# Layer 2 of a four-layer convolution network: the order of ScalarE's squares, the two relus and the projection within a turn

## The chip, the cores and the metric

The kernel runs on one core of one Trainium2 chip. The metric is the time of one execution on the device in microseconds (us); the median of three executions of the kernel before is 8452.17 us (8451.48 to 8460.17). The core has five engines that run side by side, each working through its own instructions in order: TensorE (PE, with its weight loads apart as PEld), VectorE (DVE), ScalarE (ACT), GpSimd (POOL) and SyncE (SP). SP computes nothing here; it issues all of the kernel's transfers between memory and the core. Engines wait for each other and for transfers by semaphores.

## The reference

The input x has 16 images of 64 x 64 pixels with 256 channels. Four layers follow each other, each as x + layer(norm(x)): a linear attention, a channel and spatial gate with a state scan and a batch norm, a 3 x 3 involution (layer 2 in this text, the third in order) and a 7 x 7 involution (layer 3). What matters here, cut to layer 2 and its neighbours:

```
# layer 1 ends: x2 is the gated map, normed over the batch, with a relu
x = x + relu((x2 - mean) * rsqrt(var + EPS) * bn_gamma + bn_beta)
# layer 2: v = group norm of x (32 groups, mean and variance per image)
r  = relu(((v @ Wr + br) - mean) * rsqrt(var + BN_EPS) * gamma + beta)  # kernel branch, 64 wide
w  = (r @ Ws + bs)            # 9 weights for each of 16 groups and each pixel
xi = v @ Wi + bi              # projection, 256 channels, zero-padded by one pixel
out[pixel, c] = sum over the 9 neighbours k of w[pixel, group(c), k] * xi[neighbour k, c]
x = x + out
# layer 3 begins with the group norm of this x
```

Everything is float32.

## The kernel before

Layer 2's stage is one long list of turns, written out by hand inside `tc.manual_schedule()` (line 1204): each engine carries out its instructions in the order in which the program names them. An image is cut into eight chunks of 512 pixels (NCH, CT). In turn n four jobs run on four different chunks, by the lags of line 1184, `LAG = (0, 12, 20, 31)`, with the function `jobs` (1187) turning a turn's number into images and chunks:

- *end* (lag 0): layer 1's last step, `end_of_layer1` (965), a generator in three parts. VectorE makes two multiplies (975, tiles z and pf); ScalarE takes the relus of both (981) and GpSimd adds them to x1, which gives x2 (985), and x2's store is noted; ScalarE squares x2 with a running sum (992, tile sq). When an image's last chunk is squared, `norm2` is begun (999): the group norm of the image in small steps, one step at each call of `step()`, which also scales the layer's weights by the norm.
- *proj* (lag 12): `projected` (1031). TensorE multiplies x2 by the projection (1038, px), ScalarE writes it with its bias into pad (1042), a padded image with one row of border; the last chunk of an image also copies two border rows (1049, 1050).
- *inv* (lag 20): the involution. One turn ahead of it, `prepare` (1236) makes what it needs: `reduced2` (1052) is the kernel branch's product (1059, pr) and relu (1062, rt); `patches` (1075) transposes the padded lines on TensorE (1084, pt) and copies them in nine pieces on ScalarE (1088, xs), with the first half of the weights (1069, pw) made behind the first three copies through the argument `between`. In its own turn VectorE multiplies patches and weights in two halves (`products`, 1107, pd), the first half is summed on GpSimd (1120, 1121) and the second on VectorE (1261), and the residual, transposed by TensorE (`residual`, 1093, lo), is added by VectorE (1231 for the first half, in the next turn, and 1263 for the second). The result is x3.
- A turn later (*made*), `turned` (1123) transposes x3 back (1133) and ScalarE copies it with a running sum (1134, c3), and `statistics3` (1150) squares it on ScalarE (1154). An image's last chunk begins `norm3` (1161), the same small steps for layer 3's norm.
- *cen* (lag 31): `centred` (1172) loads x3 again, subtracts the group means on GpSimd (880, cen) and notes twelve stores to strips, the layout that layer 3 reads.

The image's first patches need the border rows that the projection of the same image's last chunk writes. So in the turn before an image's first involution chunk (an *image's first turn* in the change's words, `nxt[1] == 0`), `prepare` stands behind `projected`, and in all others ahead of it.

SP issues, in each turn: loads for the next turn (942: x2p, x2r, two of x1, two of pf), stores noted in the turn before (1213: x2, twelve of strips, two of x3, two of c3), and four loads of xc for the next turn's centring (942). Tiles are double-buffered, x2r and x3 threefold. TensorE's results for px, pr, pt and the norms' small products share three PSUM buffers (tag tr).

ScalarE's order in an ordinary turn before is: two relus of layer 1, the kernel branch's relu, nine xs copies, two c3 copies, two pads, layer 3's two squares, layer 1's two squares. In an image's first turn it is: two relus of layer 1, two c3 copies, two pads with the border copies, the kernel branch's relu, nine xs copies, four squares.

Of the kernel before, what the change touches and what calls it, by code (L numbers as in the profile page):

```python
# [19 lines left out]
NCH = 8  # L20
# [16 lines left out]
def network(ctx: ExitStack, tc: tile.TileContext, a: dict, out: bass.AP):  # L37
    nc = tc.nc
    NI = a["x"].shape[0]
# [859 lines left out]
    with ExitStack() as st:  # L899
# [29 lines left out]
        for b in range(2):  # L929

            rt = bconst(f"rt{b}", [65, CT])
# [33 lines left out]
        def end_of_layer1(i, rc):  # L965

            if rc == 0:
                st0[i] = [
                    wk.tile([P, 2, NCH], F32, tag=f"st0{k}", name="st0") for k in range(2)
                ]  # L970
            sums, squares = st0[i]
            x1, pf = taken("x1"), taken("pf")
            zs = [wk.tile([P, 2, 256], F32, tag="z", name="z", bufs=1), pf]
            for h, z in enumerate(zs):
                nc.vector.scalar_tensor_tensor(
                    z, x1[:, h], ngm1[:, i, h : h + 1], pf, ALU.add, ALU.mult
                )
            yield
            x2 = wk.tile([P, 2, CT], F32, tag="x2", name="x2")
            for h, z in enumerate(zs):  # L980
                nc.scalar.activation(
                    z, z, AF.Relu, bias=bnp[:, 1, h : h + 1], scale=ab[:, 0, i, h : h + 1],
                    accum_out=sums[:, h, rc : rc + 1],
                )
                nc.gpsimd.tensor_tensor(
                    x2[:, h].rearrange("p (t g) -> p g t", g=2), z, x1[:, h], ALU.add
                )
            stores.append((x2_d[i, rc], x2))
            yield
            sq = wk.tile([P, CT], F32, tag="sq", name="sq", bufs=1)  # L990
            for h in range(2):
                nc.scalar.activation(
                    sq, x2[:, h], AF.Square,
                    bias=ngm1[:, i, h : h + 1], accum_out=squares[:, h, rc : rc + 1],
                )
            if rc == NCH - 1:
                begun.append(norm2(i))
# [54 lines left out]
        def reduced2(i, rc):  # L1052

            wrs, b2, _, _ = gn2[i]
            rt = rts[rc % 2]
            x2 = taken("x2r")
            pr = tr.tile([P, CT], F32, tag="tr", name="pr")
            for h in range(2):
                nc.tensor.matmul(
                    pr[0:64, :], lhsT=wrs[:, h, :], rhs=x2[:, h], start=(h == 0), stop=(h == 1)  # L1060
                )
            nc.scalar.activation(rt[0:64, :], pr[0:64, :], AF.Relu, bias=b2, scale=sb2[0:64, 0:1])  # L1062
            return x2, rt

        def weights(rt, oh):

            pw = pwp.tile([P, 4, 72], F32, tag="pw", name="pw")
            for r in range(4):
                nc.tensor.matmul(
                    pw[:, r], lhsT=rt[:, r * P : (r + 1) * P], rhs=ws[:, oh * 72 : oh * 72 + 72],  # L1070
                    start=True, stop=True,
                )
            return pw

        def patches(i, rc, between):


            xs = xs_p.tile([P, 6, 3, C], F32, tag="xs", name="xs")
            for j in range(3):
                for e in range(0, 6, 2):  # L1080
                    pt = tr.tile([P, 2, C], F32, tag="tr", name="pt")
                    for k in range(2):
                        for h in range(2):
                            nc.tensor.transpose(  # L1084
                                pt[:, k, h * P : (h + 1) * P],
                                lines[:, h, rc * 4 + e + k, 2 * j : 2 * j + P], ident,
                            )
                    nc.scalar.copy(xs[:, e : e + 2, j, :], pt)  # L1088
                if j == 0:
                    between()  # L1090
            return xs
# [31 lines left out]
        def turned(i, rc, x3):  # L1123

            if rc == 0:
                st3[i] = [
                    wk.tile([P, 2, NCH], F32, tag=f"st3{k}", name="st3") for k in range(2)
                ]
            c3 = wk.tile([P, 2, 2, 256], F32, tag="c3", name="c3", bufs=2)
            for oh in range(2):  # L1130
                pt = tr.tile([P, 4, P], F32, tag="tr", name="pt")
                for r in range(4):
                    nc.tensor.transpose(pt[:, r, :], x3[:, r, oh * P : (oh + 1) * P], ident)
                nc.scalar.activation(
                    c3[:, oh], pt.rearrange("p r t -> p (r t)").rearrange("p (t g) -> p g t", g=2),
                    AF.Copy, accum_out=st3[i][0][:, oh, rc : rc + 1],
                )
            x3n = x3_d[i].rearrange("(g r w) c -> g w r c", g=2, w=HW)
            for g in range(2):
                stores.append((x3n[g][:, rc * 4 : rc * 4 + 4], x3[g:P:2]))  # L1140
            for h in range(2):
                stores.append((
                    c3_d[i, :, h].rearrange("p (g t) -> p g t", g=2)[
                        :, :, rc * 256 : rc * 256 + 256
                    ],
                    c3[:, h],
                ))
            return c3
# [23 lines left out]
        def centred(i, rc):  # L1172
            cen = wk.tile([P, 4, 4, 64], F32, tag="cen", name="cen")
            stores.extend(centred_strips(i, rc, taken("xc"), cen, gmb[i]))
# [6 lines left out]

        LAG = (0, 12, 20, 31)
        TURNS = NI * NCH + 23

        def jobs(n):

# [14 lines left out]

        with tc.manual_schedule():
            loads(0)
            ahead, made = None, None
            for n in range(TURNS):
                end, proj, inv, cen = jobs(n)
                nxt = jobs(n + 1)[2]
                done, stores[:] = list(stores), []  # L1210
                loads(n + 1)
                for dst, src in done:
                    nc.sync.dma_start(out=dst, in_=src)
                nxt_cen = jobs(n + 1)[3]
                if nxt_cen:
                    load_centred(*nxt_cen)
                now, ahead = ahead, None
                ending = end_of_layer1(*end) if end else None
                if ending:
                    next(ending)  # L1220
                    next(ending)
                if cen:
                    centred(*cen)
                step()
                for c in begun:
                    next(c)
                chains.extend(begun)
                begun.clear()
                if made:
                    half = made[2][:, :, 0:P]  # L1230
                    nc.vector.tensor_tensor(half, half, made[3], ALU.add)
                if inv:
                    w1 = weights(now[1], 1)
                    x3 = wk.tile([P, 4, C], F32, tag="x3", name="x3", bufs=3)

                def prepare():
                    x2r, rt = reduced2(*nxt)
                    ahead = [x2r, rt]
                    ahead.append(patches(*nxt, lambda: ahead.append(weights(rt, 0))))
                    return ahead  # L1240

                if nxt and nxt[1]:
                    ahead = prepare()
                if inv:
                    los = residual(now[0])
                c3 = turned(*made[:3]) if made else None
                step()
                if proj:
                    projected(*proj)
                if inv:  # L1250
                    pd = products(0, now[2], now[3])
                    sums_on_pool(pd, x3)
                if nxt and not nxt[1]:
                    ahead = prepare()
                if inv:
                    pd1 = products(1, w1, now[3])
                step()
                if made:
                    statistics3(*made[:2], c3)
                if inv:  # L1260
                    nc.vector.tensor_reduce(x3[:, :, P:C], pd1, AX.X, ALU.add)  # L1261
                    half = x3[:, :, P:C]
                    nc.vector.tensor_tensor(half, half, los[1], ALU.add)
                if ending:
                    next(ending, None)
                made = (*inv, x3, los[0]) if inv else None
            for dst, src in stores:
                nc.sync.dma_start(out=dst, in_=src)
# [380 lines left out]
```

## Time and profile before

| What | Value |
|---|---|
| Median of three executions | 8452.17 us (8451.48 to 8460.17) |
| The profiled execution | 8439.31 us; its span 8437.5 us |
| Busy share of the span | PE 82%, PEld 63%, DVE 71%, ACT 58%, POOL 36% |
| Layer 2's first turns, end alone or end and projection | 3419 to 3555 us |
| Its involution, from the first product to the last | 3555.7 to 6028 us |
| The two products of a turn (L1107), each | 4.95 us |
| The sum of the second half (L1261) | 4.95 us |
| The sums on GpSimd of a turn (L1120, L1121) | 8.4 to 8.5 and 1.6 to 2.0 us |
| A layer-1 relu (L981), a square (L992), each with its sum read | 0.99 us, 0.91 us |
| The kernel branch's relu (L1062), an xs copy (L1088), a pad (L1042) | 0.76 us, 0.59 us, 0.69 us |
| Granted TensorE clock, mean of the span | 0.903 |

The span is the time from the first instruction to the last one of a single profiled execution. Busy is time in which an engine has an instruction of its own under way; an engine's idle time is put down to what it waited for last. A line of the profile names the source line (L1107), the engine, the operation, and the tiles as out<-in; "SPq" is SP's queue, and its entries are the issue of a transfer, not the transfer itself.

### The profile page before, as it was taken

The page shows a single profiled execution, that of the slowest core. Times are in us where ns is not written, and L with a number is a line of the kernel's source. Part 1 is how long each engine was busy: PE and PEld are TensorE (multiplying, and loading weights), DVE is VectorE, ACT ScalarE, POOL GpSimd, SP SyncE. Part 2 cuts the span into 40 slices and gives each one's busy share as a digit, 9 for nine tenths or more (in the row PEclk, how much of TensorE's full clock was granted, in tenths as well). Part 3 has the DMA queues.
Part 4 walks back from the last instruction along what each step waited for, and adds up shares of the span by engine and source line. Part 5 has one row for each costly group of instructions (what it writes and reads, how often), then busy time and mean ns, then how long its engine had stood idle before and what let it go on. Part 6 is the DMA issues. An engine that isn't in the chain of part 4 may idle for free.

```text
span 8437.5 us, 214993 instructions
## 1 busy us (share of the span) xinstructions
PE 6919.5 (82%) x88348; PEld 5293.7 (63%) x88348; DVE 6026.7 (71%) x7071; ACT 4858.5 (58%) x11136; POOL 3065.7 (36%) x2154
## 2 busy tenths in 40 slices
PE   7888888888888776487887888788588888888887
PEld 5666666666666542265665565566477777777776
DVE  6877887787777757499999999999644444444444
ACT  3655655555565437676666666665355555555554
POOL 1222222222222100377777777777511211111112
PEclk9999999999999868688888888889699999999999
DMA  7644444434333228657777777776578788888887
GB/s 223 191 143 138 138 133 146 140 130 137 131 117 113 98 72 265 223 201 233 241 238 242 238 238 239 238 237 211 188 227 254 247 250 255 254 258 256 258 253 244
DMA packets 1081768, 1695.65 MB, mean 201 GB/s; under 512 B 138833, under 2 KB 684962, under 8 KB 1079634
## 3 DMA queue, kind: packets, MB, share of 16 engines
q1 hardware_dynamic: 1080786, 1681.90, 62.0%
q8 instruction: 696, 11.40, 0.6%
q14 instruction: 286, 2.34, 0.1%
HBM read 1234.54 MB, written 469.76 MB: 202 GB/s over the span
## 4 chain that ended last, share of the span: by engine, by line
PE 49%; DVE 19%; DMA 11%; ACT 9%; issue 7%; SPq 3%; POOL 2%; DVEq 0%; ACTq 0%; POOLq 0%
PE pk L1366 13%; PE pa L1432 8%; PE pkv L292 4%; PE pt L1084 4%; PE px L1038 4%; DMA x<-x_d 3%; DVE pd L1107 3%; PE py L423 2%; PE pq L280 2%; DMA xn<-in_x 2%; PE pctx L350 2%; PE pr L1333 2%; ACT sq L432 1%; DVE mq L387 1%; DVE x L451 1%
## 5 line engine op out<-in xcount | busy, mean ns | idle before, releaser
L1107 DVE TENSOR_TENSOR pd<-xs,pw 128x4608 f32<-128x4608 f32 x256 | 1255.8, 4946 | 42.2 <-ACT xs L1088 42.2
L1366 PE MATMUL pk<-rt,span 64*128 64x176 f32 x12288 | 1186.6, 330 | 48.4 <-issue 41.3
L1376 ACT ACTIVATE wm<-pk,spanb 128x176 f32<-128x176 f32 x2560 | 846.0, 424 | 569.0 <-PE pk L1366 566.8
L1452 POOL TENSOR_TENSOR ex<-ex,rx 128x192 f32<-128x192 f32 (+2 forms) x768 | 436.4, 570 | 1854.8 <-DVE ex L1445 1198.3
L1120 POOL TENSOR_TENSOR pd<-pd 128x2048 f32<-128x2048 f32 (+2 forms) x384 | 1075.9, 2802 | 75.6 <-DVE pd L1107 55.4
L1366 PEld LDWEIGHTS pk<-rt,span 64*128 64x128 f32 x12288 | 977.7, 193 | 129.7 <-issue 71.9
L1445 DVE SCALAR_TENSOR_TENSOR ex<-pa,msk,ex 128x192 f32<-128x192 f32 x704 | 294.3, 418 | 1040.3 <-ACT ex L1444 976.1
L292 PE MATMUL pkv<-wq,xn 128*128 128x256 f32 x4096 | 968.9, 382 | 14.5 <-ACT va L301 14.5
L1084 PE MATMUL pt<-ident,pad 128*128 128x128 f32 x4608 | 756.3, 330 | 266.7 <-ACT rt L1062 266.7
L375 POOL TENSOR_TENSOR qa<-qa,mq 128x1024 f32<-128x1024 f32 x256 | 507.5, 2005 | 1170.8 <-DVE mq L384 511.5
L1084 PEld LDWEIGHTS pt<-ident,pad 128*128 128x128 f32 x4608 | 673.9, 175 | 407.2 <-ACT rt L1062 292.6
L1381 DVE TENSOR_TENSOR wm<-pk,spanb 128x704 f32<-128x704 f32 x896 | 793.9, 888 | 189.3 <-PE pk L1366 186.4
L1432 PE MATMUL pa<-wm,xw 126*32 126x48 f32 x45056 | 754.9, 215 | 211.5 <-issue 185.6
L292 PEld LDWEIGHTS pkv<-wq,xn 128*128 128x128 f32 x4096 | 772.7, 192 | 227.1 <-issue 101.3
L1432 PEld LDWEIGHTS pa<-wm,xw 126*32 126x32 f32 x45056 | 623.5, 112 | 391.8 <-issue 333.2
L1088 ACT COPY xs<-pt 128x512 f32<-128x512 f32 x1152 | 619.4, 591 | 239.4 <-PE pt L1084 233.8
L1261 DVE TENSOR_REDUCE x<-pd 128x512 f32<-128x4608 f32 x128 | 633.4, 4949 | 2.2 <-DVE gm L140 0.3
L1038 PE MATMUL px<-x2p,wis 128*128 128x512 f32 x1024 | 519.3, 653 | 111.8 <-issue 63.8
L280 PE MATMUL pq<-xn,wq 128*128 128x512 f32 x1024 | 526.2, 629 | 95.1 <-DVE xn L166 77.1
L423 PE MATMUL py<-wo,o 128*128 128x256 f32 x2048 | 527.6, 413 | 32.3 <-DVE maps L510 28.6
L423 PEld LDWEIGHTS py<-wo,o 128*128 128x128 f32 x2048 | 488.9, 310 | 65.3 <-issue 39.1
L1444 ACT ACTIVATE ex<-pa,msk 128x192 f32<-128x192 f32 x704 | 299.4, 425 | 388.6 <-PE pa L1432 189.1
(234 smaller groups left out, 11879.3 us busy)
## 6 DMA issues: line engine op xcount, KB each, us to landing
xw<-strips SPq DMA_DIRECT2D x1408, 256.0 KB
xn<-in_x SPq DMA_DIRECT2D x256, 512.0 KB
x_d<-x SPq DMA_DIRECT2D x256, 512.0 KB
xin<-in_x SPq DMA_DIRECT2D x128, 512.0 KB
x<-in_x SPq DMA_DIRECT2D x128, 512.0 KB
xm<-x_d SPq DMA_DIRECT2D x128, 512.0 KB
x<-x_d SPq DMA_DIRECT2D x128, 512.0 KB
x<-x_d SPq DMA_DIRECT2D x256, 256.0 KB
```

What stands on the lines that cost most here:

```text
L280: nc.tensor.matmul(pq, lhsT=wq[:, h, f0 : f0 + P], rhs=xn[:, h], start=(h == 0), stop=(h == 1),)
L292: nc.tensor.matmul(pkv[:, q], lhsT=xn[:, h, q * P : (q + 1) * P], rhs=wq[:, h, f0 + P : f0 + 384], start=(h == 0), stop=(h == 1),)
L423: nc.tensor.matmul(py[:, q, :], lhsT=om[i, hf][:, :, ch * 4 + q], rhs=wo[:, hf, :], start=(hf == 0), stop=(hf == 1),)
L1038: nc.tensor.matmul(px, lhsT=w[:, h, fh * P : (fh + 1) * P], rhs=x2[:, h], start=(h == 0), stop=(h == 1),)
L1084: nc.tensor.transpose(pt[:, k, h * P : (h + 1) * P], lines[:, h, rc * 4 + e + k, 2 * j : 2 * j + P], ident,)
L1107: nc.vector.tensor_tensor(pd.rearrange("p r (g f) k -> p r g f k", f=16), run, pw.rearrange("p r (g k) -> p r g k", k=9).unsqueeze(3).broa ...
L1120: nc.gpsimd.tensor_tensor(pd[..., 0:n], pd[..., 0:n], pd[..., n : 2 * n], ALU.add)
L1261: nc.vector.tensor_reduce(x3[:, :, P:C], pd1, AX.X, ALU.add)
L1366: nc.tensor.matmul(pkv[:, b, m], lhsT=span[half, first + gg, s0 : s0 + P], rhs=rto[half, o // 4 * 2 + m, :], start=True, stop=True,)
L1376: nc.scalar.activation(dst[:, m // 2, m % 2], pkv[:, m // 2, m % 2], AF.Identity, bias=spanb[:, g0 + m : g0 + m + 1],)
L1381: nc.vector.tensor_tensor(dst, pkv, spanb[:, g0 : g0 + 4].rearrange("p (b m) -> p b m", b=2).unsqueeze(3).broadcast_to([P, 2, 2, NTL]), AL ...
L1432: nc.tensor.matmul(pav[p0 : p0 + 32, :, tj * TC : (tj + 1) * TC].rearrange("c g (w v) -> c g w v", v=2), lhsT=xw[0:TILE_IN, k, tj, 32 * q ...
```

## The change

The lags of projection, involution and centring grow by one, and one turn is added. Layer 1's squares of a chunk (`squares`) now run one turn after its relus: behind the first three xs copies of `patches` and the weights' first half ("the heads"), or, where there is nothing to prepare, behind the relus. In an ordinary turn the kernel branch's relu (in `reduced2`) comes first on ScalarE, and layer 1's relus, with GpSimd's sums and the centring, follow it (`relus`, called from `prepare`). In an image's first turn the order is: relus, projection, preparation, and then the residual and the turned chunk. Layer 3's squares follow directly on `turned`, ahead of the projection's pads. GpSimd's sums of the first half stay before the second product.

```diff
-        LAG = (0, 12, 20, 31)
-        TURNS = NI * NCH + 23
+        LAG = (0, 13, 21, 32)
+        TURNS = NI * NCH + 24
...
-            ahead, made = None, None
+            ahead, made, ending = None, None, None
...
-                ending = end_of_layer1(*end) if end else None
+                squares, ending = ending, end_of_layer1(*end) if end else None
                 if ending:
                     next(ending)
-                    next(ending)
-                if cen:
-                    centred(*cen)
                 step()
...
-                def prepare():
+                def relus():
+                    if ending:
+                        next(ending)
+                    if cen:
+                        centred(*cen)
+
+                def prepare(other):
                     x2r, rt = reduced2(*nxt)
+                    other()
                     ahead = [x2r, rt]
-                    ahead.append(patches(*nxt, lambda: ahead.append(weights(rt, 0))))
+
+                    def between():
+                        ahead.append(weights(rt, 0))
+                        if squares:
+                            next(squares, None)
+
+                    ahead.append(patches(*nxt, between))
                     return ahead
 
-                if nxt and nxt[1]:
-                    ahead = prepare()
+                first = nxt and not nxt[1]
+                if first:
+                    relus()
+                    projected(*proj)
+                    ahead = prepare(lambda: None)
+                elif nxt:
+                    ahead = prepare(relus)
+                else:
+                    relus()
+                    if squares:
+                        next(squares, None)
                 if inv:
                     los = residual(now[0])
-                c3 = turned(*made[:3]) if made else None
+                if made:
+                    statistics3(*made[:2], turned(*made[:3]))
                 step()
-                if proj:
+                if proj and not first:
                     projected(*proj)
                 if inv:
                     pd = products(0, now[2], now[3])
                     sums_on_pool(pd, x3)
-                if nxt and not nxt[1]:
-                    ahead = prepare()
-                if inv:
                     pd1 = products(1, w1, now[3])
                 step()
-                if made:
-                    statistics3(*made[:2], c3)
                 if inv:
                     nc.vector.tensor_reduce(x3[:, :, P:C], pd1, AX.X, ALU.add)
                     half = x3[:, :, P:C]
                     nc.vector.tensor_tensor(half, half, los[1], ALU.add)
-                if ending:
-                    next(ending, None)
                 made = (*inv, x3, los[0]) if inv else None
```

## The prediction

> **What bounds the kernel now.** The change touches layer 2 alone, and there I read four views in this order: busy time by stretch, VectorE's waits, SP's queue in order of time, and SP's own waits. Layer 2's products run from 3555.7 to 6028 us. Its long middle, where all its jobs overlap, is turns 44 to 123 (ten images of eight turns, from one stalled first product to another, 4013.7 to 5627.4). Busy time there (columns: stretch, length, then busy us of PE, PE weight loads, VectorE, ScalarE, GpSimd, granted clock, DMA share, GB/s):
>
> ```profile
> 4013.70:5627.40 1613.70, 1287.31 (x6642) 964.20 (x6642) 1514.85 (x821) 1046.80 (x2301) 1219.39 (x580) 0.85 0.73 239
> ```
>
> A turn takes 1613.7/80 = 20.17 us, and VectorE is busy for 94% of it. That suggests that VectorE binds and that its remaining waits are the price. Its waits there (us in total, times, longest):
>
> ```profile
> DVE pd L1107 <- ACT xs L1088: 32.2, 10, 4.0
> DVE isq L93 <- PE pv L151: 14.3, 10, 1.8
> DVE mom L114 <- ACT sq L992: 10.0, 10, 1.5
> DVE mom L114 <- ACT sq L1154: 9.3, 9, 1.8
> ```
>
> The diff aims at lines 1, 3 and 4: 51.5 us. But VectorE's need is well below 20.17 us. Undisturbed turns (21, 22, 26) take 17.55 us, and the two group norms add some 3 us per image: 8 x 17.55 + 3 = 143 us, where an image takes 161.4. The rest is about 8 us of waits and about 10 us of VectorE instructions that run long: the two layer-1 multiplies of a turn (L975) take 0.75 us each when alone and up to 2.0 beside GpSimd's sums. So something else sets 20.17. SP's queue, one turn of it:
>
> ```profile
> 4455.11 0.40 SPq L942 DMA_DIRECT2D x2p<-x_d  x1
> 4455.56 0.43 SPq L942 DMA_DIRECT2D x2r<-x_d  x1
> 4456.10 1.31 SPq L942 DMA_DIRECT2D x<-x_d  x2
> 4457.51 1.09 SPq L942 DMA_DIRECT2D pf<-fac_d  x2
> 4458.64 0.65 SPq L1213 DMA_DIRECT2D x_d<-x  x1
> 4459.41 10.39 SPq L1213 DMA_DIRECT2D strips<-cen  x12
> 4469.91 1.30 SPq L1213 DMA_DIRECT2D x_d<-x  x2
> 4471.31 1.10 SPq L1213 DMA_DIRECT2D c_d<-c  x2
> 4472.46 2.62 SPq L942 DMA_DIRECT2D xc<-x_d  x4
> 4475.18 0.40 SPq L942 DMA_DIRECT2D x2p<-x_d  x1
> ```
>
> 27 transfers follow each other without a hole, and the next turn's x2p comes 20.07 us after this one's. The transfers carry eight semaphores in rotation, and each waits until the one eight places before has landed. SP's waits in the same ten images:
>
> ```profile
> SPq L1213 <- DMA xc<-x_d: 62.7, 106, 1.2
> SPq L1213 <- DMA x2r<-x_d: 47.9, 80, 1.6
> SPq L1213 <- DMA x2p<-x_d: 46.2, 78, 1.4
> ...
> SPq L942 <- PE px L1038: 2.4, 4, 0.7
> ```
>
> SP waits for its own transfers (157 us, 2 per turn). The remaining rows, some 78 us in pieces of at most 1.4 us, mostly name engine work that no transfer touches (copies of xs, rt), so I take them for landings put down to a neighbour. The one engine whose work a load needs shows 2.4 us in 80 turns. SP is saturated, and no engine holds it up. How that reaches VectorE (GpSimd in order of time):
>
> ```profile
> 4479.81 2.36 POOL L880 TENSOR_TENSOR cen<-xc,gmb 128x1024 f32<-128x1024 f32 x1 [4.07 <-DMA x2p<-x_d]
> 4482.12 8.44 POOL L1120 TENSOR_TENSOR pd<-pd 128x2048 f32<-128x2048 f32 x3
> 4490.64 1.97 POOL L1121 TENSOR_TENSOR x<-pd 128x512 f32<-128x512 f32 x1
> ```
>
> xc, SP's last load of a turn, was issued by 4475.08 and landed 4.7 us later; then cen, then the sums, until 4492.61; VectorE adds the residual (L1231) at 4493.09 and may multiply from 4493.8. So a turn's products can't begin before 18.7 us after the last issue of xc. Set against that floor, the products of turns 36 to 126 start 0.0 to 6.4 us after it, never before. Each image touches the floor (0.0 to 1.3 us above) in its turn 3 mod 8, is thrown up by the xs wait, and sinks back. SP's own turn length doesn't follow that distance: 20.22 us in 19 turns within 1 us of the floor, 20.15 in 27 turns more than 4 us above it.
>
> **What the Trainium skill says.** "Perfetto Trace Analysis", section What "DMA-bound" means, lists as a separate bound the sequencer that issues, recognised by a track of solid DMA slices, which are descriptor generation and not movement. This trace agrees: SP solid, DMA share only 0.73. "SBUF — State Buffer", section Who interferes with whom, says that a VectorE instruction with two SBUF inputs contends with GpSimd's reads: here 0.75 against up to 2.0 us (L975). "DMA: Bandwidth & Descriptors", section Issuing engines are not separate DMA queues, says that issue time is usually small beside the transfer; here the measurement says otherwise, 0.67 us of issue for strips pieces of 36 to 128 KB.
>
> **The change part by part.** No instruction and no transfer is added or removed; SP's and GpSimd's orders within a turn are the old ones (x2's store, strips, x3 and c3; sums into x2, cen, products' sums).
>
> *First turns (line 3 of PE's order).* Before, PE in turn 67 waited for the residual's PSUM and then 5.19 us more until px at 4484.04 (VectorE's L1028 had just read the small result before it), so xs was complete at 4498.2 and the products came 4.05 us late. Now px follows w1 and the relus. Relus end at 4474.3, px done by then, two pads of 0.69 and two edge copies of 0.31 end at 4476.3; rt 0.76, nine copies at 0.59 to 0.85, 1.82 of squares: about 4484 to 4487, before the floor at 4493.8. Wait gone: 32.2 us in ten images. What is late next there is L1231, held by GpSimd's sums at the floor.
>
> *Squares.* The layer-1 squares (2 x 0.91 us) go behind the first three copies of the next turn, and layer 3's pair in front of the pads, into ScalarE's idle time before them (301.5 us in 80 turns waiting for px, 3.8 a turn). The moments (L114) then find them done: 19.3 us gone. Behind the squares are six xs copies and PE's transposes; they end about 10 us before the next products in ordinary turns, and that covers 1.82 us. Without this cover it would be 1.82 a turn.
>
> *Kernel branch's relu first.* rt needs only PE's pr; it now precedes the layer-1 relus, of which the x2 sums on GpSimd and so cen are waiting. In turn 63 ScalarE reached the relus at 4413.6 through 3.6 us of squares; now pr ends at 4412.3, rt near 4413.0, and the multiply at 4412.5. Relus no later: zero, covered by the removed squares, else 0.76 a turn.
>
> *One turn more.* Projection, products and centring each lag one turn further behind layer 1. A filling turn costs (3549.39 - 3443.34)/18 = 5.9 us; a full turn of 20.2 drops out, since layer 1's and centring's loads overlap in one turn less; one draining turn of 16.1 (turns 136 and 137) is added: +1.8.
>
> *What is left as a gain.* Before SP fills up (turns 20 to 31) VectorE does bind: waits of the moments 0.42 + 0.35 + 1.20 = 2.0 us. SP's waits for px, 2.4 x 95/80 = 2.9 us over some 95 full turns. The other savings only bring VectorE down to the floor earlier. Sum: +1.8 - 2.0 - 2.9 = **-3.1 us** against the profiled execution's 8439.3 us (span 8437.5), so 8436; carried to the median, 12.9 higher, **8449 us**.
>
> Unknown: whether landings come sooner or later with engines in other phase. The two means above differ by 0.07 us, so I take none, and +-0.1 us a turn, x 95 = +-10, as its bounds. With the spread of the runs (8451.5 to 8460.2), the likeliest case has 8434 to 8466.
>
> **Rivals.** *A: VectorE binds after all.* For it: 94% busy, and the chain of waits runs through ScalarE and PE too. Then the waits are saved, 51.5, and the long multiplies of the turn after each first turn, 10 x 1.8 = 18: 69.8 x 97/80 = 85 us, 2.0 before, and the extra turn costs 5.9 - 1.5: about 8370. Against it: the floor, and SP's indifference. If SP's landing waits shrank in part, the time lies between.
>
> *B: slower, through SP's head.* The load of x2p for turn n+1 waits until px of turn n-1 has read its buffer. Near the floor px ended 9 us before SP got there (4466 against 4475.18); 6 us above it they meet (4516.27 and 4516.29, turn 69). ScalarE's pads now come behind 1.8 us of squares. If px is held 1.8 us longer and VectorE still rides high in four turns of eight, SP loses 1.8 x 4 x 12 = 86 us, half of it 43: 8495. It decides from px held past SP's arrival by 0.18 us in the mean turn (17 us). Against: without the xs wait VectorE doesn't ride high.
>
> *C: the edit misses.* xs stays late in first turns because the relus, put first, wait for VectorE's multiplies. Costless at the floor: 8452, as now.
>
> **How the numbers follow.** Forecast 0.62, C 0.06, A with its part gains 0.20, B 0.12. 0.2% is 17 us, about what a measurement here can tell from none: faster 0.20, same 0.68, slower 0.12. The range: the likeliest's 8434 to 8466, down to 8400 for part gains and up to 8476 for a small B.
>
> **What would show it.** Right: VectorE's waits for xs and for the squares nearly gone, its waits for GpSimd's sums (7.7 us in these ten images) and cen's waits for DMA larger, SP's turn still 20.0 to 20.3 us, products within about 2 us of the floor throughout. A is right if SP's turn falls below 19.5; B if SP waits for px in many turns. I am wrong altogether if SP shows holes and VectorE's waits still vanish.

## The result, and the profile after

The changed kernel takes 8463.99 us (median of 12 executions, 8445.27 to 8477.87); the kernel before, on the same chip, 8457.28 us (12 executions, 8446.66 to 8462.88). The ratio is 1.0009, with a 95% interval of 1.0000 to 1.0018, so a difference of 0.2% lies outside it. The forecast was 8449 with "no change" at 0.68.

The same ten images as before (turns of the middle, here from 4036.8 to 5647.4 us), busy time by stretch (stretch, length, then busy us of PE, PE weight loads, VectorE, ScalarE, GpSimd, granted clock, DMA share, GB/s):

```profile
4036.80:5647.40 1610.60, 1243.08 (x6640) 889.82 (x6640) 1555.68 (x822) 1023.82 (x2301) 1230.89 (x581) 0.89 0.72 239
```

A turn takes 1610.6/80 = 20.13 us, where it took 20.17. What stands out is VectorE: busy for 1555.7 us instead of 1514.9, with the same work. Its waits in this stretch (us in total, times, longest):

```profile
DVE b L1026 <- PE pm L1020: 24.7, 9, 4.2
DVE x L1228 <- POOL x L1121: 9.2, 6, 1.5
DVE gmb L869 <- PE pb L864: 8.0, 10, 0.8
DVE isq L93 <- PE pv L151: 0.9, 2, 0.6
```

The waits for xs and for the two kinds of squares are gone, and the one for pv fell from 14.3 to 0.9. A new one has come: the norm's small result b waits for pm, which TensorE now makes behind an image's first patches. So 65 us of waits were saved and 25 came. SP's queue, one turn in order of time:

```profile
4499.34 2.61 SPq L942 DMA_DIRECT2D xc<-x_d  x4
4502.05 0.40 SPq L942 DMA_DIRECT2D x2p<-x_d  x1
...
4507.02 9.77 SPq L1213 DMA_DIRECT2D strips<-cen  x12
4516.90 1.28 SPq L1213 DMA_DIRECT2D x_d<-x  x2
4518.27 1.10 SPq L1213 DMA_DIRECT2D c_d<-c  x2
4519.43 2.63 SPq L942 DMA_DIRECT2D xc<-x_d  x4
```

It is as solid as before: xc comes back after 20.09 us. SP's own waits in the ten images, where no row names px any more:

```profile
SPq L1213 <- DMA xc<-x_d: 55.0, 90, 1.2
SPq L1213 <- DMA x2p<-x_d: 44.8, 77, 1.4
SPq L1213 <- DMA x2r<-x_d: 44.7, 79, 1.2
```

How that reaches VectorE, in the turn after xc's issue at 4501.95, first GpSimd and then VectorE in order of time:

```profile
4507.29 2.38 POOL L880 TENSOR_TENSOR cen<-xc,gmb 128x1024 f32<-128x1024 f32 x1 [4.86 <-DMA x2r<-x_d]
4509.64 8.75 POOL L1120 TENSOR_TENSOR pd<-pd 128x2048 f32<-128x2048 f32 x3
4518.47 1.96 POOL L1121 TENSOR_TENSOR x<-pd 128x512 f32<-128x512 f32 x1
```

```profile
4517.24 1.70 DVE L975 SCALAR_TENSOR_TENSOR pf<-x,ngm,pf 128x512 f32<-128x512 f32 x1
4520.47 0.69 DVE L1228 TENSOR_TENSOR x<-x,lo 128x512 f32<-128x512 f32 x1 [1.53 <-POOL x L1121]
4521.07 9.81 DVE L1107 TENSOR_TENSOR pd<-xs,pw 128x4608 f32<-128x4608 f32 x2
```

cen stands 4.86 us for its transfer, the sums end at 4520.43, VectorE waits 1.53 us for them and multiplies 19.1 us after xc's issue. It is the turn of an image's first chunk, the one that waited 4.05 us for xs before. Over 90 full turns the products now start 1.75 us after the floor of 18.7 us, where they started 2.76 us after it.

One thing was not in the forecast. The norms' small instructions (128 x 2 elements), in the groups of the ten images, before and then after (the number after the bar is busy us, then mean ns of one):

```profile
L121 DVE TENSOR_TENSOR mom<-gn_mv,ngm 128x2 f32<-128x2 f32 x20 | 3.2, 161 | 0.7
L118 DVE SCALAR_TENSOR_TENSOR gn_mv<-mom,mean 128x2 f32<-128x2 f32 x10 | 1.5, 150 | 0.0
L122 DVE TENSOR_TENSOR mom<-mom 128x2 f32<-128x2 f32 x20 | 4.2, 212 | 0.7
```

```profile
L121 DVE TENSOR_TENSOR mom<-gn_mv,ngm 128x2 f32<-128x2 f32 x20 | 23.9, 1194 | 0.7
L118 DVE SCALAR_TENSOR_TENSOR gn_mv<-mom,mean 128x2 f32<-128x2 f32 x10 | 10.3, 1033 | 0.0
L122 DVE TENSOR_TENSOR mom<-mom 128x2 f32<-128x2 f32 x20 | 8.4, 420 | 0.7
```

An instruction of 0.16 us takes 1.2. It has moved beside GpSimd's layer-1 sums (L985), which take 1.27 us each. L121, L118 and L122 account for 33.7 of VectorE's 41 us more.

Over the whole of layer 2, from the first multiply (L975) to the last product, the profiled execution takes 2613.1 us against 2608.8. The rest of the 29.7 us between the two spans lies in layers whose code is the same (15.8 ahead of layer 2, 9.6 behind it). I take it for the spread of single executions: the part ahead of layer 2 took 3410 to 3435 us in the profiles of seven kernels whose code is the same up to there.

### The profile page after: what moved, and what is told of

It reads as the page before. It is cut to its first block, busy times and chain, and to the rows that moved or that the text cites. A ratio compares the mean times of both kernels' runs of the same rounds, so it can differ in the third digit from the quotient of the medians.

```text
span 8467.2 us, 214899 instructions
## 1 busy us (share of the span) xinstructions
PE 6869.9 (81%) x88348; PEld 5190.6 (61%) x88348; DVE 6077.2 (72%) x7071; ACT 4826.2 (57%) x11136; POOL 3076.3 (36%) x2154
## 5 line engine op out<-in xcount | busy, mean ns | idle before, releaser
L1084 PE MATMUL pt<-ident,pad 128*128 128x128 f32 x4608 | 724.4, 318 | 347.8 <-ACT xs L1088 308.2
L1084 PEld LDWEIGHTS pt<-ident,pad 128*128 128x128 f32 x4608 | 606.5, 164 | 530.4 <-ACT xs L1088 354.0
L1088 ACT COPY xs<-pt 128x512 f32<-128x512 f32 x1152 | 596.0, 590 | 50.3 <-PE pt L1084 46.8
```

Of the source, the lines that this page charges most:

```text
L1084: nc.tensor.transpose(pt[:, k, h * P : (h + 1) * P], lines[:, h, rc * 4 + e + k, 2 * j : 2 * j + P], ident,)
```

## The experiments

Two theories. **S**: SP's queue sets the turn, and VectorE's saved waits only bring it down to the floor. **E**: the order of the engines sets the turn, and what the change saved was eaten by the new collisions and by the wait for pm. In what follows, "turn" is the time from one turn's products to those 80 turns later, over 80, in the ten images; "stretch" is from the first products to the last, 2472.4 us before and 2468.5 after.

### Fewer and more transfers, the same bytes

The edits: pf's two loads in one, c3's two stores in one (25 transfers a turn, in both kernels); x1's two loads in one as well (24; for this x1's two halves lie beside each other in memory, which also changes the addresses of its other transfers); two loads of 1 KB added to the 27 (29).

```diff
-            load("pf", [P, 2, 256], *(
-                (lambda t, g=g: t[:, g], facr[i, tks[g]].partition_broadcast(P)) for g in range(2)
-            ))
+            both = facr[i].rearrange("(g t) -> g t", g=2)[:, rc * 256 : rc * 256 + 256]
+            load("pf", [P, 2, 256], (lambda t: t, both.partition_broadcast(P)))
...
-            for h in range(2):
-                stores.append((
-                    c3_d[i, :, h].rearrange("p (g t) -> p g t", g=2)[
-                        :, :, rc * 256 : rc * 256 + 256
-                    ],
-                    c3[:, h],
-                ))
+            stores.append((
+                c3_d[i].rearrange("p h (g t) -> p (h g) t", g=2)[:, :, rc * 256 : rc * 256 + 256],
+                c3.rearrange("p h g t -> p (h g) t"),
+            ))
```

```diff
-            load("x1", [P, 2, 2, 256], *(
-                (lambda t, g=g: t[:, :, g], x1_d[i, :, :, tks[g]].rearrange("h p t -> p h t"))
-                for g in range(2)
-            ))
+            load("x1", [P, 2, 2, 256], (
+                lambda t: t.rearrange("p h g t -> p (h g) t"),
+                x1_d[i].rearrange("p h (g t) -> p (h g) t", g=2)[:, :, rc * 256 : rc * 256 + 256],
+            ))
```

```diff
                 load_layer1(*end)
+            for k in range(2):
+                nc.sync.dma_start(
+                    out=wk.tile([P, 2], F32, tag=f"tiny{k}", name="tiny", bufs=2), in_=a["bi"]
+                )
```

> The changed kernel, with two of the 27 transfers of a layer-2 turn merged into others of the same queue: the two halves of pf are loaded by one transfer, and the two halves of c3 are stored by one. Bytes, engines' work and outputs stay. Theory S (SP's queue sets the turn at 20.15 us, about 0.75 us for each transfer): the queue could do 25 transfers in 18.7 us, so VectorE takes over with some 19.4 us a turn (1555.7 us busy in 80 turns): 0.7 us x 90 turns = 60 us faster than the changed kernel, about 8400. Theory E (the engines' order sets the turn, and what the change saved was eaten by the new collisions of small VectorE instructions with GpSimd's sums and by the new wait for pm): nothing, 8455 to 8470, the turn stays at 20.1.

> The kernel before with the same two merges. Theory S: the queue falls to 18.7 us a turn, and VectorE with its waits binds: 18.9 us busy, 0.4 for xs, 0.25 for the moments, 0.2 for isq, some 19.8 us: 0.4 us x 90 turns = 35 us faster than before, about 8420, and some 20 to 30 us behind the changed kernel with the same merges, so that the change now shows. Theory E: no gain, 8450 to 8460, and no distance to the changed kernel with the merges.

> As the changed kernel with two merges, and the two halves of x1 in one transfer too (x1's scratch has its halves beside each other, so that layers 0 and 1 use other addresses in the same transfers): 24 transfers a turn. Theory S: the queue could do 17.9 us, VectorE binds already at 25, so within 10 us of the changed kernel with two merges; if VectorE does not bind yet, a further 0.7 us a turn, 60 us. Theory E: nothing, within 10 us of the changed kernel.

> The changed kernel with two more transfers a turn on SP's queue, 1 KB each (bi into a scratch tile that nobody reads). Theory S: each takes its place in the queue, 0.65 to 0.75 us: 2 x 0.7 x 93 turns = 130 us slower, about 8590, the turn at 21.5. Theory E: SP has room, so within 10 us of the changed kernel.

| Kernel | Transfers a turn | Median, us | Ratio to before, 95% | Turn, us |
|---|---|---|---|---|
| changed, 25 | 25 | 8443.8 | 0.9984 (0.9972 to 0.9996) | 19.97 |
| before, 25 | 25 | 8443.3 | 0.9988 (0.9976 to 1.0000) | 20.04 |
| changed, 24 | 24 | 8523.1 | 1.0080 (1.0060 to 1.0100) | 20.82 |
| changed, 29 | 29 | 8635.0 | 1.0211 (1.0193 to 1.0229) | 21.68 |

Two loads of 1 KB, which nobody reads, cost 21.68 - 20.13 = 1.55 us a turn, 0.78 each: SP has no room, and E falls as an account of the full load, since it allowed 10 us and some 170 came. But two transfers merged into others gave 0.16 us, not 0.7; the two kernels stay level (8443.8 and 8443.3 us), where S expected 20 to 30 us between them; and a third merge *cost* time. So the number of transfers is not the whole of it. The issue of pf with 25 transfers, and SP's waits for landings (for the end of an earlier transfer) in the ten images:

```profile
4501.12 0.40 SPq L942 DMA_DIRECT2D pf<-fac_d  x1
```

```profile
SPq L1209 <- DMA xc<-x_d: 78.8, 171, 1.1
SPq L1209 <- DMA x_d<-x: 50.5, 80, 2.0
SPq L1209 <- DMA x2r<-x_d: 50.2, 80, 1.4
SPq L1209 <- DMA x2p<-x_d: 30.1, 80, 0.9
```

pf's issue takes 0.40 us instead of 1.80, as hoped. The waits for landings took it back: 209.6 us in these four rows, against 144.5 in the three above. SP has no wait for px in these ten images, so VectorE doesn't set the turn here either. At most eight transfers are under way at a time; when two become one, each of the eight carries more, and I take it that it lands later for that (the profile doesn't show the landings themselves). A turn of 27 transfers gives each 8 x 20.13/27 = 5.97 us until the one eight places behind it may go; with 29 it is 5.98, with 25 6.39, with 24 6.94. In the run with 24, the merged load of x1 (512 KB) is what SP waits for, 116.0 us in 80 turns.

Another count fits these runs better than the number of transfers: the profile's packets, the pieces in which the DMA engines move a transfer. The ten images with 27 transfers and then with 29:

```profile
DMA packets 307870, 385.40 MB, mean 239 GB/s; under 512 B 21110, under 2 KB 277038, under 8 KB 307758
DMA packets 331147, 385.83 MB, mean 222 GB/s; under 512 B 44162, under 2 KB 300312, under 8 KB 331032
```

That is 191.2 and 190.9 packets a us, and 191.1 with 25 transfers (305189 packets), while GB/s changed by 7%. A load of 1 KB brings some 145 packets, a merge takes away some 17. At 191 packets a us that comes to 1.52 us for the two loads (1.55 measured) and 0.18 for the two merges (0.16 measured). The run with 24 doesn't fit (182.3). Packets were not varied by themselves, so this is an account that fits, not a cause that was shown.

### Fewer bytes, and fewer transfers with them

Layer 2's strips get three columns of each neighbour (eight of the twelve stores). The first edit leaves these eight out, in both kernels; the second keeps all 27 transfers and makes the eight one column wide. The columns that nobody writes then hold zeros, which layer 0 stores (up to seven small stores at a time, where it had three). The diff is cut, with the values put in for the arguments that select them.

```diff
-            for u0, u1, w0, dt in ((0, TC, 3, 0), (TC - 3, TC, 0, 1), (0, 3, TC + 3, -1)):
+            for u0, u1, w0, dt in ((0, TC, 3, 0), (TC - 3, TC, 0, 1), (0, 3, TC + 3, -1))[:1]:
...
+            for u0, u1, w0, dt in ((0, TC, 3, 0), (TC - 1, TC, 2, 1), (0, 1, TC + 3, -1)):
```

> The changed kernel, leaving out of layer 2 the eight transfers of a turn that copy three columns of cen to the neighbouring strips (the strips' side columns hold zeros instead, written in layer 0 where SP waits for TensorE; layer 3 reads as much as before). 19 transfers a turn are left on SP. Theory S (SP's queue with eight transfers in flight sets the turn): the queue falls below 17 us, VectorE binds at its own 19.4 us plus 0.1 of waits: the stretch from the first to the last products falls from 2468 to about 2410, 60 us. Theory E (the engines' order sets it): the turn stays at 20.1, the stretch at 2460 to 2470.

> The kernel before, with the same eight transfers of a turn left out. Theory S: VectorE with its waits binds at 18.9 + 0.85 = 19.8 us: the stretch falls from 2472 to about 2435, and the change is worth 20 to 30 us between these two, where it was worth nothing with all transfers. Theory E: 2465 to 2475, and no distance to the changed kernel with 19 transfers.

> The changed kernel with all 27 transfers of a turn, but the eight side copies one column wide instead of three (16 KB each instead of 48 KB; zeros in the other columns from layer 0, as in the run with 19 transfers). If theory S holds by the number of transfers, the turn stays within 0.2 us of 20.15. If it holds by how long the eight in flight take to land, the turn falls by the 8 x 32 KB that no longer move, at 239 GB/s some 1.1 us, down to VectorE's 19.5. Theory E: nothing.

| Kernel | Median, us | Ratio to before, 95% | Turn, us | Stretch, us |
|---|---|---|---|---|
| changed, narrow | 8300.3 | 0.9840 (0.9825 to 0.9855) | 19.11 | 2377.0 |
| changed, 19 | 8312.4 | 0.9860 (0.9842 to 0.9877) | 19.33 | 2400.1 |
| before, 19 | 8243.0 | 0.9776 (0.9761 to 0.9790) | 18.65 | 2333.6 |

Busy time by stretch, the narrow run (27 transfers):

```profile
3985.40:5513.80 1528.40, 1239.40 (x6640) 881.32 (x6640) 1487.54 (x822) 1016.95 (x2301) 1208.15 (x581) 0.89 0.75 240
```

A turn of 20.13 us at 239 GB/s moves 4.81 MB in the changed kernel, and one of 19.11 us at 240 GB/s 4.59 MB here: 5% fewer bytes, 5% less time, with the same number of transfers. SP waits for px 11 times only (13.7 us in all), so the queue still sets most of the turn. The number of transfers alone does not set it, then: what they carry counts too. Whether that counts by bytes or by packets stays open, since the narrow stores have fewer of both (295668 packets, 193.4 a us). As an account of the full load E is out: with the transfers relieved the stretch of both kernels shrinks, by 138.8 us (before), 68.4 (changed) and 91.5 (changed, narrow). The ratios in the table overstate this. In the profiled executions with 19 transfers the layers ahead of layer 2 took 29.5 and 43.4 us less (before, changed), and those behind it 29.2 and 40.5 less, than with 27. Why was not tested.

VectorE doesn't feel the queue as a wait alone. It is busy for 96.6% of the ten images in the changed kernel and for 97.3% in the narrow one, but its busy time goes with the queue's load too: z and pf (L975) together took 203.6 us with 27 transfers, 137.5 in the narrow run and 119.7 with 19. That is most of why the kernel before fell to 18.65, below the 19.8 expected: its z and pf, whose length I had kept, shrank from 192.2 to 136.0 us.

The two kernels with 19 transfers hold the surprise. With the queue out of the way the change is worth not 20 to 30 us of gain: it *costs* 69.4 us (8312.4 - 8243.0; the intervals of the ratios are far apart). Busy time by stretch, before with 19 and then changed with 19:

```profile
3962.70:5454.50 1491.80, 1264.77 (x6630) 957.92 (x6631) 1447.82 (x822) 1044.08 (x2294) 1204.59 (x580) 0.87 0.72 240
```

```profile
3985.00:5531.70 1546.70, 1223.45 (x6640) 891.44 (x6640) 1523.38 (x822) 1019.66 (x2301) 1200.24 (x581) 0.89 0.70 231
```

VectorE is busy for 97 and 98.5% of it, and SP now waits for px, before and then changed: the queue has room, VectorE binds.

```profile
SPq L949 <- PE px L1045: 387.8, 70, 10.5
SPq L949 <- PE px L1045: 433.5, 70, 11.5
```

VectorE's waits are 31.9 us before and 11.2 after (all rows of each), 20.7 saved. Its busy time grew by 1523.38 - 1447.82 = 75.6. The difference, 54.9, is that of the two lengths, to the tenth.

### Where VectorE's time goes: the norm beside GpSimd's sums

One norm in the changed kernel with 19 transfers, VectorE and then GpSimd in order of time (line numbers stand 7 higher):

```profile
4774.68 1.20 DVE L121 TENSOR_TENSOR mom<-gn_mv,ngm 128x2 f32<-128x2 f32 x1
4775.92 1.20 DVE L122 TENSOR_TENSOR mom<-mom 128x2 f32<-128x2 f32 x1
4777.15 2.27 DVE L123 SCALAR_TENSOR_TENSOR gn_mv<-mom 128x2 f32<-128x2 f32 x1
```

```profile
4774.60 1.27 POOL L992 TENSOR_TENSOR x<-z,x 128x512 f32<-128x512 f32 x1 [1.94 <-DMA x<-x_d]
4775.82 1.27 POOL L992 TENSOR_TENSOR x<-pf,x 128x512 f32<-128x512 f32 x1
4777.06 2.35 POOL L887 TENSOR_TENSOR cen<-xc,gmb 128x1024 f32<-128x1024 f32 x1
```

Three times VectorE's instruction begins 0.08 to 0.10 us after one of GpSimd's and ends 0.01 to 0.03 us after it. It doesn't run slowly, it is held until GpSimd's is through: 4.67 us for three instructions of 0.16. The Trainium skill, "SBUF — State Buffer", section Who interferes with whom, names both sides of this: a VectorE instruction with two SBUF inputs contends with GpSimd's reads, and "Issue order, not op shape, decides who blocks." This trace agrees: 128 x 2 elements wait for 128 x 1024. In the kernel before with 19 transfers GpSimd's sum begins 0.57 us after L121 in most norms (14 of 20), when L123 is done, and nothing is held (VectorE, then GpSimd):

```profile
4877.49 0.16 DVE L121 TENSOR_TENSOR mom<-gn_mv,ngm 128x2 f32<-128x2 f32 x1
4877.69 0.16 DVE L122 TENSOR_TENSOR mom<-mom 128x2 f32<-128x2 f32 x1
4877.89 0.16 DVE L123 SCALAR_TENSOR_TENSOR gn_mv<-mom 128x2 f32<-128x2 f32 x1
4878.08 1.28 POOL L992 TENSOR_TENSOR x<-z,x 128x512 f32<-128x512 f32 x1 [2.31 <-ACT z L988]
```

In five of the others the sum begins later still, and in one L121 is held (1.19 us).

Two kernels follow, both with 19 transfers. The first moves the norms' first step ahead of z and pf, out of the sums' way. The second undoes one part of the change, the place of layer 1's squares.

```diff
                 squares, ending = ending, end_of_layer1(*end) if end else None
+                fresh = list(begun)
+                begun.clear()
+                for c in fresh:
+                    next(c)
                 if ending:
                     next(ending)
                 step()
-                for c in begun:
-                    next(c)
-                chains.extend(begun)
-                begun.clear()
+                chains.extend(fresh)
```

```diff
                     def between():
                         ahead.append(weights(rt, 0))
-                        if squares:
-                            next(squares, None)
...
+                if ending:
+                    next(ending, None)
                 made = (*inv, x3, los[0]) if inv else None
```

> The changed kernel with 19 transfers on SP's queue as before (side copies left out of layer 2), and the first step of the norms (VectorE's small instructions from the moments' sums to gn_mv) moved ahead of the kernel branch's two VectorE instructions of layer 1 (z and pf), so that it lies before GpSimd's layer-1 sums and not beside them. Theory K (with the queue relieved VectorE binds, and the change costs its time by putting these small instructions beside GpSimd's sums: 1.2 us in place of 0.16): some 78 us of 80 turns go, the turn falls from 19.3 to 18.4, the stretch from first to last products from 2395 to about 2310, the whole to about 8230, at or below the 8243 of the kernel before with 19 transfers. If something else of the change costs the 69 us between those two (projection first, the wait for pm, the relus' order): the turn stays at 19.2 to 19.4, 8300 or more.

> The changed kernel with 19 transfers, with one part of the change undone: layer 1's squares stand at the end of their own turn again, so that the moments of the norm wait for them. Theory K: the wait returns (some 12 us in ten images) and holds the small instructions back past part of GpSimd's sums, so that the norm's instructions are shorter again: the turn falls from 19.3 to 18.6 to 18.9, the whole to 8250 to 8275. If the squares have nothing to do with the collisions, the turn grows by the wait, to 19.4, and the whole to 8325.

The norm ahead: 8227.2 us, ratio 0.9769 (0.9753 to 0.9786), turn 18.34, stretch 2299.6. The busy time by stretch and two groups:

```profile
3963.20:5430.50 1467.30, 1188.45 (x6640) 854.69 (x6640) 1442.95 (x821) 1016.47 (x2301) 1201.61 (x581) 0.93 0.73 244
```

```profile
L123 DVE SCALAR_TENSOR_TENSOR gn_mv<-mom 128x2 f32<-128x2 f32 x20 | 3.2, 161 | 0.7
L121 DVE TENSOR_TENSOR mom<-gn_mv,ngm 128x2 f32<-128x2 f32 x20 | 3.2, 161 | 0.7
```

VectorE's busy time falls by 80.4 us in 80 turns, and the turn by 1.0 us. Only that step was moved, so the collisions are shown to be the change's price (a fourth small instruction of the norms, L148, lies later and still takes 24.4 us in both changed kernels, against 5.3 in the kernel before). Without them the changed order is 24.5 us shorter in the ten images than the kernel before with 19 transfers (1467.3 against 1491.8), about the waits that it saves; between the whole executions the ratios, 0.9769 and 0.9776, don't tell the two apart.

The squares back: 8319.0 us, ratio 0.9885 (0.9867 to 0.9902), turn 19.47. That is the second branch of its expectation: the place of layer 1's squares doesn't make the collisions, and L121 to L123 take 1.2 to 2.3 us as before. I then took ScalarE as the cause. In the kernel before with 19 transfers the relu of z (L988) begins 0.7 to 3.9 us after z is written at the norms, since ScalarE is still at its squares; in the changed one 0.03 to 0.28 us after it, and GpSimd's sums follow the relu. So the last run puts both kinds of squares back:

```diff
-                if made:
-                    statistics3(*made[:2], turned(*made[:3]))
+                c3 = turned(*made[:3]) if made else None
...
+                if made:
+                    statistics3(*made[:2], c3)
```

> The changed kernel with 19 transfers, with ScalarE's squares of both kinds (layer 1's and those of the layer's result) back at the end of their turn; the relus' order, projection first and the extra turn stay as changed. Theory K2 (the collisions come because ScalarE, freed of the squares, starts the relu of z 0.04 us after z is written where it was some 1 to 2 us late, which starts GpSimd's sums beside the norm's small instructions instead of behind them): ScalarE is late again, the norm's instructions take 0.16 to 0.3 us, the turn falls from 19.3 to 18.6 to 18.8, the whole to 8240 to 8260. If the order of the relus or the projection does it, the turn stays at 19.3 to 19.5, 8310 to 8330.

It takes 8350.8 us, ratio 0.9879 (0.9863 to 0.9896), turn 19.37: no relief. ScalarE reaches the relu 0.03 to 0.12 us after z here too, and L121 to L123 take 0.74, 1.16 and 1.80 us. K2 falls as far as it names the squares. What is shown is that the sums' start beside the norm costs the time. Which of the parts left (the relus' order, the projection first, the extra turn) brings ScalarE to the relu at least 0.6 us sooner wasn't tried and stays open.

### Another queue, and the norm moved under the full load

The eight side stores of a turn are issued by ScalarE:

> The changed kernel with the eight side copies issued by ScalarE in the middle of the next turn, in place of SP at its start: same bytes, same results. ScalarE is busy 11 of 20 us, and gets some 8 x 0.6 = 5 us more. Theory S: as with 19 transfers, a turn of some 19.5 us, 50 us faster than the changed kernel, about 8410, unless ScalarE's issues make the patches late: then its turn grows and VectorE shows waits for xs. Theory E: the same as the changed kernel or slower, by ScalarE's 5 us.

```diff
+                side = [d for d in done if len(d) == 3]
...
+                for dst, src, _ in side[:4]:
+                    nc.scalar.dma_start(out=dst, in_=src)
                 if proj and not first:
                     projected(*proj)
+                for dst, src, _ in side[4:]:
+                    nc.scalar.dma_start(out=dst, in_=src)
```

8478.9 us, ratio 1.0058 (1.0038 to 1.0078), where S expected some 8410. ScalarE now stands in the rotation of eight as well. Its waits in the ten images:

```profile
ACT rt L1063 <- DMA strips<-cen: 220.5, 54, 10.6
ACT pad L1043 <- DMA strips<-cen: 96.1, 37, 4.5
```

The turn falls to 19.76 us in the ten images, but the rest of the stretch grows, to 2487.0 in all. "Perfetto Trace Analysis", section DMA Optimizations, says that balancing over the engines that can issue may help where descriptor generation binds. Here it did not, over the whole: what SP waited for is landing, and ScalarE, an engine with work to do, now waits for it too.

The changed kernel with 25 transfers and the norm ahead (both edits as above):

> The changed kernel, all its work done, with the two merges (25 transfers) and the norms' first step ahead of z and pf. Theory S (SP's queue with eight in flight binds at 20.0 us here): the collisions are hidden in saturated turns, so only the first 11 turns gain, some 5 to 10 us: about 8435. If the collisions do set the time of saturated turns too: 0.5 us x 90 turns more, about 8390.

8421.8 us, ratio 0.9999 (0.9988 to 1.0009), turn 20.01: nothing was gained on the whole. In the first 11 turns, where VectorE binds, the expected gain is there (199.7 us, against 204.4 without the move). In the ten images the run decides nothing between S and the collisions, because the move didn't take them away: VectorE is busy for 1545.5 us, against 1547.0, since the norm's later instructions are now held beside other sums (L122 went from 7.4 to 16.1 us, L147 from 3.2 to 13.6). The two kernels with 25 transfers are the fastest measured of those that do the whole work, 0.16% (changed) and 0.12% under the kernel before, with no difference between them.

## Why the prediction was right

The likeliest case came, and in the main by its mechanism: the queue sets the turn of the middle, and saved waits there gave nothing. The terms beside it were less right. Point by point:

- **What bounds.** "SP is saturated, and no engine holds it up": shown for the changed kernel by the run with two loads of 1 KB (171 us) and by the narrow run. The turn stayed at 20.13, inside 20.0 to 20.3; cen's waits for transfers grew (its four rows, one of them named issue, from 107.8 to 265.2 us); VectorE's wait for the sums went from 7.7 to 9.2, which is little. Products came within 2 us of the floor in the mean, not throughout, as the prediction had it: up to 4.2 us above it in the ten images, and 5.9 at the start.
- **What the queue's bound is.** Here the reading was half right. It quoted issue time, solid slices, as the bound, and called 0.67 us of issue not small without the transfer's own time beside it (by its own lines xc landed 4.7 us after its issue). The run with 25 transfers took away issue time and got more waiting for landings for it. The bound is eight in flight until they land; whether bytes or packets set how long that is stays open.
- **First turns and squares.** Gone, as worked out: 32.2 and 19.3 us of waits. Not foreseen: pv's wait went too (14.3 to 0.9), and pm's came (24.7), since pm is made behind the first turn's patches.
- **Kernel branch's relu, "zero".** It asked whether the relus come later. They came *earlier* (0.04 us after z at the norms of the ten images, where it had been 1.0 to 5.3), and the step stops there. It should have asked what GpSimd's earlier sums run into: VectorE's small instructions, +40.8 us busy in the ten images. The floor hid this.
- **One turn more, +1.8.** Filling took 8.2 us more (5.9 expected).
- **What is left as a gain, -2.0 and -2.9.** SP's waits for px are gone, as said. The 2.0 us came with the other sign. In turns 20 to 30, where VectorE binds, 198.9 us became 204.4: the moments' waits are gone, but at the first norm (ahead of the products of turn 24, now turn 25) L121 takes 1.21 us and L122 1.20 beside sums of 1.27 and 1.28. Sum: -3.1 was predicted for layer 2, +4.3 was measured in one execution each.
- **Rival A** had 85 us of gain if VectorE binds (its 51.5 and 18 make 69.5, so 84). With VectorE bound the change costs 69 us. Its error is the same missing term: it counted waits and took "long multiplies" as something that the change could only remove.
- **Rivals B and C**: no wait of SP for px, and xs is not late. Neither happened.

The forecast of "no change" thus didn't rest on the size of the saved waits, and that is what kept it right. That the time saved (65 us) and the time added (66 us) nearly cancel would suit E as well; what decides against it are the runs with 29 transfers and with narrow stores. The single terms that the prediction added up to -3.1 us are too small for these measurements to confirm.

## What to carry to other kernels

Before an engine's waits are priced, look for the resource that fixes the period. Here it was SP's queue of transfers: its turn stayed at 20.1 to 20.2 us, through 65 us of saved waits and 66 us of new waits and collisions. A full queue is tested with two tiny transfers, and it may be full of landings rather than issues: here smaller stores helped, while two merges gave 0.16 us, a third cost time, and another queue didn't help. When a wait on one engine is taken away, look at what its neighbour now does at the same moment: here small VectorE instructions that slid beside GpSimd's sums were held to the end of these, and with the queue relieved that made the change 69 us slower instead of faster.

## What was unexpected of the hardware

- A VectorE instruction of 128 x 2 elements, 0.16 us alone, took 1.20 us beside a GpSimd sum of 128 x 512 and 2.27 us beside one of 128 x 1024, ending 0.01 to 0.03 us behind it each time.
- Two loads of 1 KB cost 0.78 us of a turn each, though their issue is 0.40 us; the rate fell from 239 to 222 GB/s with them, but the packets a us stayed at 191.
- The merged load of 512 KB (four pieces of 1 KB for each partition, at equal distance) in place of two of 256 KB, together with x1's other place in memory, made the turn longer, 20.82 against 19.97 us. Which of the two does it was not tested; nor was what keeps the eight in flight at 222 to 241 GB/s, or at some 191 packets a us.
